# One pool of short-lived tiles, seven weight buffers, keys ordered by part, and a first norm turned by VectorE through DRAM

## The chip, the cores and the metric

The kernel runs on one core of a Trainium2 chip. A core has TensorE (PE in the profile; PEld is its weight load), VectorE (DVE), ScalarE (ACT), GpSimd (POOL) and SyncE (SP), which here only issues DMA transfers. Tiles lie in SBUF (128 partitions) or in PSUM, where matmuls write; PSUM has eight banks of 128 x 512 fp32 values. Transfers between DRAM and SBUF run on 16 DMA engines. The metric is the device time of one execution in microseconds.

## The reference

A transformer block in fp32 over x of shape (16, 512, 512): 16 batches of 512 tokens with 512 features. It has two halves, each a norm, a function, another norm and a residual.

```python
x = x + layernorm(attn(layernorm(x)))
x = x + layernorm(ffn(layernorm(x)))

# attn: 16 heads of 32; low-rank projections
q = h @ Wq_down.T @ Wq_up.T            # 512 -> 384 -> 512
c = h @ Wkv_down.T                     # 512 -> 128
k, v = c @ k_up[head], c @ v_up[head]  # 128 -> 32 per head
scores = q @ k.T * SCALE - slope[head] * |i - j|, causal
out = softmax(scores) @ v @ Wo.T

# ffn: weights are fp4 numbers, 8 to an int32, with a scale per group of 128
gate, up = h @ W_gate_up.T             # 512 -> 2 x 1408
y = (silu(gate) * up) @ W_down.T       # 1408 -> 512
y / sqrt(mean(y * y) + 1e-6)
```

## The kernel before

**The planner.** The code does not issue instructions where it describes them. Each piece of work is a `task`: the engines that may run it with an assumed busy time and end (`act`, `dve`, `pe`, `dma(us)`), a function that issues it, a due time in units of batches, and the tiles that it reads, writes or holds. `Plan.run` is a list scheduler. Again and again it takes the task that could start first by its assumed times, and among those the one with the earliest due time, looking at most half a batch ahead (`window=0.5`). What comes out is one fixed order of instructions per engine. On the chip every engine follows its order and waits on semaphores. A task that either ScalarE or VectorE can do (`either`) goes to the one that is free first in the plan. Buffers belong to named pools (`SLOTS`): `buf("g", ...)` takes a slot of pool `g` when its first task is placed and gives it back after its last; a later user of a slot waits for the earlier one's readers.

**The work of a batch.** A batch is four tiles of 128 tokens; attention has four groups (`g`) of four heads, and the queries are taken in four blocks (`qb`), each with (qb + 1) x 128 keys because of the causal mask.

- `first_norm`: `xl` is loaded, VectorE takes its statistics (L450), GpSimd the reciprocal root, ScalarE or VectorE normalizes in place. TensorE transposes the tile in four 128 x 128 pieces into a PSUM bank (`pta`, L490), and ScalarE or VectorE copies this into `xnT` (L439), which holds features on partitions and the 512 tokens along each.
- `project` (L600): `pc`, `pq`, `pk`, `pv` are the matmuls for c, q, k and v. Their results are copied out of PSUM.
- `scores`: four small matmuls side by side on rows of the array (`s`, L680); one VectorE operation adds the distance term and finds the maximum (L692); ScalarE does the exponential and the row sum (L707) into `p`.
- `turn`: brings `p` to keys on partitions, `pT`. In batch 0 by TensorE transposes (L773). In all later batches VectorE turns blocks of 32 x 32 in place (L790), one DMA stores the tile to DRAM (`pd`, L792), and four DMAs load it so that the blocks come to their places (`pT`, L797).
- `attend`: matmuls on columns of the array (`po`, L820), and a multiplication by the inverse row sums `rb`, which also go by way of DRAM (L741, L746).
- `tail`: the output projection (`pw`, L848), two norms, transposes (`ptf`) and a split of the result into two parts, `x2`.
- `ffn`: for each of 11 steps of 128 hidden features and for gate and up, a weight tile `wi` is loaded from DRAM (L891, 256 KB); each of four feature chunks gets two matmuls (`pg`, `pu`, L900); ScalarE scales and copies every first bank (L914), VectorE adds every second (L921), GpSimd adds the two halves (L927). ScalarE's tanh, one VectorE operation (L937) and a product on GpSimd (L941) make the hidden tile `hT`. Then 44 products `py` (L949), statistics, the last norm, and a store by GpSimd's queue.

In batch 0 the packed weights are unpacked as well and written to DRAM as `w_gu`.

**What sets the order around the change.** The feed-forward part of a batch is spread over the attention of the next: its due times begin 1.45 batches after the batch's start. So `wi`, `pd`, `pT`, `rb`, `xl` and `x` transfers are all issued by SyncE, one after another, in the planned order; one that waits holds those behind it. The short-lived tiles have pools of their own: `y` (3; also `rb`, scales and a raw load), `g`, `u`, `sum`, `th` (2 each). `wi` has four buffers.

Of the kernel before, what the change touches and what calls it, by code (L numbers as in the profile page):

```python
# [252 lines left out]
def dma(us):  # L253
    return 450.0, us * 1000.0
# [4 lines left out]
def attn_ffn_kernel(  # L259
# [38 lines left out]
        "xnT": (1, [P, ND, L], F32),  # L298
# [5 lines left out]
        "y": (3, [P, D], F32),  # L304
        "x2": (1, [P, 2, ND, L], F32R),
        "hT": (1, [P, NI, L], F32),
        "g": (2, [P, L], F32),
        "u": (2, [P, L], F32),
        "sum": (2, [P, L], F32),
        "th": (2, [P, L], F32),  # L310
        "wi": (4, [P, ND * P], F32R),
        **{f"p{qb}": (1, [P, (qb + 1) * P // HD, HPG, HD], F32) for qb in range(NT)},
        **{f"pT{qb}": (1, [P, qb + 1, HPG, HPG, HD], F32) for qb in range(NT)},
# [22 lines left out]


# [15 lines left out]
    dist = fixed([P, L], "dist")  # L353
# [10 lines left out]

    task({POOL: pool2(L)}, make_dist, -0.1, writes=[dist])

# [59 lines left out]
    raw = buf("y", "raw")  # L426
# [10 lines left out]

    def copy(e, dst, src):
        (nc.scalar.copy if e == ACT else nc.vector.tensor_copy)(dst, src)  # L439

    def either(n, extra=0.0):
        return {ACT: act(n, extra), DVE: dve(n, extra)}
# [12 lines left out]
    def norm(dst, src, rd, wr, tag, due, dur):  # L455

        st, mv, r, f = stats(src, tag, due)
        task({DVE: (700.0 + 150, 1000.0)}, f, due, reads=rd, writes=[st, mv])
        task({POOL: (1100.0, 1200.0)},
             lambda e: (rsqrt(r.t[:, 0:1], mv.t[:, 1:2], EPS_LN), shift(r, mv)), due,  # L460
             reads=[mv], writes=[r])
        scaled(dst, src, mv, r, rd, wr, due, dur)
# [87 lines left out]
    def unpack_gate_up(i):  # L550
        due = 0.15 + 0.06 * i
        words, high = unpack(gup, i * 16, NGU * P, i % (NI // 2) * 2, due)
        for half in range(2):
            wi = buf("th", f"wq_{i}_{half}")
            cols = slice(half * ND * P, (half + 1) * ND * P)
            task({ACT: act(ND * P)},
                 lambda e, wi=wi, cols=cols: nc.scalar.activation(
                     wi.t.bitcast(F32R), high()[:, cols], AF.Copy, scale=2.0**14),
                 due, reads=words, writes=[wi])
            task({SP: dma(2.6)},  # L560
                 lambda e, wi=wi, half=half: nc.sync.dma_start(w_gu[i, half], wi.t),
                 due, reads=[wi], writes=[(gu, (i, half))])

    def unpack_down(i):
        due = 0.85 + 0.06 * i
        sc = buf("y", f"sc_{i}")
# [13 lines left out]
    xnT = {}  # L580

    def first_norm(b, t):
        due = b - 0.3 + 0.06 * t
        if t == 0:
            xnT[b] = buf("xnT", f"xnT_{b}")
        xl, xn_t = xls[b, t], xnT[b]
        norm(lambda: xl.t, lambda: xl.t, [xl], [xl], f"a_{b}_{t}", due, dve(512, -100))
# [3 lines left out]
            lambda e: copy(e, xn_t.t[:, :, t * P : (t + 1) * P], blocks(pt.t)),  # L591
# [16 lines left out]
    def make_c(m):  # L608
        m.c = buf("cT", f"cT_{m.b}")
        project(  # L610
            m.c, None, lambda c: w_kv.t[:, c, :], lambda c: m.xn.t[:, c, :], ND,
# [4 lines left out]
    def make_q(m, g, due):  # L616
# [3 lines left out]
        def put(e, pm):  # L620
# [7 lines left out]
            lambda c: m.xn.t[:, c, :], ND, [w_q, m.xn, qscale],  # L628
# [3 lines left out]
    def make_k(m, g, due):  # L632
# [4 lines left out]
            lambda e, pm: copy(e, k.t, pm),  # L637
# [16 lines left out]
    def runs(ap):  # L654
        return ap.rearrange("p (b c) -> p b c", c=HD)

    def flat(ap):
        return ap.rearrange("p b j c -> p (b j c)")


    def part(m, p, j):
        if m.b == 0:
            ap = flat(p.t)
            w = ap.shape[1] // HPG
            return runs(ap[:, j * w : (j + 1) * w])
        return p.t[:, :, j, :]

    def scores(m, g, qb, due):
# [8 lines left out]
        def f(e):  # L677
            for j in range(HPG):
# [4 lines left out]
                    k.t[rows, :w],  # L683
# [5 lines left out]
        for j in range(HPG):  # L689
# [3 lines left out]
                    part(m, p, j),  # L693
                    runs(s[j].t[:, :w]),
                    runs(dist.t[:, L - w :]),
# [6 lines left out]
                due, reads=[s[j], dist], writes=[(p, j), (nmx, j)],  # L702
            )
        for j in range(HPG):
# [3 lines left out]
                    part(m, p, j), part(m, p, j), AF.Exp, bias=nmx.t[:, j : j + 1],  # L708
# [21 lines left out]
    def inverse(m, g, due):  # L730
        r = rowsums[g]
        d = rows_d[g]
        rb = m.rb[g] = buf("y", f"rb_{m.b}_{g}")
# [27 lines left out]
    def turn(m, g, qb, p, due):  # L761
        w = (qb + 1) * P
        row = w * HPG
        name = f"{m.b}_{g}_{qb}"
        p_t = buf(f"pT{qb}", f"pT_{name}")
        if m.b == 0:

            for j in range(HPG):
                pt = buf("bank", f"pt_{name}_{j}")

                def f(e, j=j, pt=pt):
                    for kb in range(qb + 1):
                        nc.tensor.transpose(  # L773
                            pt.t[:, kb * P : (kb + 1) * P],
                            flat(p.t)[:, j * w + kb * P : j * w + (kb + 1) * P],
# [7 lines left out]
                        e, p_t.t[:, : qb + 1, :, j, :],  # L783
                        pt.t[:, :w].rearrange("p (k a c) -> p k a c", a=HPG, c=HD),
# [3 lines left out]
            return p_t  # L788
        d = scratch[g, qb]
        task({DVE: dve(row, 0.07 * row)}, lambda e: nc.vector.transpose(flat(p.t), flat(p.t)),  # L790
             due, reads=[p], writes=[p])
        task({SP: dma(5.5 + w / 200)}, lambda e: nc.sync.dma_start(d.t, flat(p.t)), due,  # L792
             reads=[p], writes=[d])
        for i in range(HPG):
# [3 lines left out]
                    p_t.t[i * HD : (i + 1) * HD, : qb + 1],  # L798
                    bass.AP(
                        d.t.tensor, d.t.offset + i * P,  # L800
                        [[row, HD], [HPG * P, qb + 1], [HD * row, HPG], [1, P]],
# [4 lines left out]
        return p_t  # L806


    def attend(m, g, units, due):
# [5 lines left out]
        def f(e):  # L815
            for q, p_t, _ in units:
                for kb in range(q + 1):
                    for j in range(HPG):
# [4 lines left out]
                            p_t.t[:, kb, :, j, :],  # L823
# [14 lines left out]
    def tail(m, t, due):  # L838
# [5 lines left out]
        pm, y = buf("bank", f"pw_{b}_{t}"), buf("y", f"y_{b}_{t}")  # L844
# [35 lines left out]
    def ffn(m):  # L880
# [3 lines left out]
        for i in range(NI):  # L884
            accs = []
            for half, kind in enumerate("gu"):
                acc = buf(kind, f"{kind}_{b}_{i}")
                add = buf("sum", f"{kind}2_{b}_{i}")
                wi = buf("wi", f"wi_{b}_{i}_{half}")
                task({SP: dma(4.5)},  # L890
# [41 lines left out]
            th = buf("th", f"th_{b}_{i}")  # L932
# [11 lines left out]
        for t in range(NT):  # L944
# [34 lines left out]
            z, x = buf("th", f"z_{b}_{t}"), m.x[t]  # L979
# [9 lines left out]
    for b in range(B):  # L989
# [22 lines left out]
        for n in range(NG * NT):  # L1012
# [3 lines left out]
            units.append((qb, turn(m, g, qb, p, due + 2.2 * STEP), None))  # L1016
# [69 lines left out]
```

## Time and profile before

| | |
|---|---|
| median of 3 runs | 2503.35 us (2502.45 to 2506.34) |
| the profiled execution | 2499.75 us, span 2498.0 us |
| mean granted TensorE clock | 0.989 |
| TensorE busy | 2407.1 us, 13496 matmul instructions |
| VectorE, ScalarE, GpSimd busy | 1825.3, 1489.8, 1190.2 us |
| DMA | 487103 packets, 497.15 MB; SyncE's queue 71.8% of 16 engines' span |
| TensorE, 906 to 1057 us | 148.76 of 151.00 us busy |

An fp32 matmul is issued as two matmul instructions, so counts in the profile are doubled for `py`, `pw`, `pq`, `pc`, `pk`, `pv`, `s` and `po`. Matmuls are pipelined: one of 512 columns is shown with 592 ns, but eight `pq` in the chain take 3.43 us. So busy time is not a measure of TensorE at its peak, and the waits that it stood in are read beside it. A batch takes about 151 us in the middle of the span.

The page gives busy time by engine, the chain of work that ended last with the share of each line, groups of instructions with what ended the idle time before them, and DMA. Other views list who waited for whom, with the total, the number and the longest; SyncE's queue has its own list, marked SPq, and idle time there costs nothing unless a transfer behind it is late.

### The profile page before, as it was taken

Reading aid. Unit: us, or ns where it says so; the run is one execution under the profiler, and the core shown is the slowest. Engines: PE = TensorE matmul, PEld = TensorE weight load, DVE = VectorE, ACT = ScalarE, POOL = GpSimd, SP = SyncE. Lnnn points to the kernel's source line nnn. Section 1 sums busy time; section 2 is a strip of 40 time slices with the busy share of each in tenths; the row PEclk is TensorE's granted clock in tenths of the full one; section 3 lists DMA queues with packets and bytes.
Section 4 is the critical chain, followed back from the end, with each engine's and each line's share of the span. In section 5 each row is a group of like instructions: output and inputs, shape, how many; then the busy total and the mean of one; then the engine's idle time right before and its main releaser. Section 6 shows DMA issues by size and latency. Waiting matters only on the chain.

```text
span 2498.0 us, 42338 instructions
## 1 busy us (share of the span) xinstructions
PE 2407.1 (96%) x13496; PEld 1347.3 (54%) x13496; DVE 1825.3 (73%) x4216; ACT 1489.8 (60%) x3516; POOL 1190.2 (48%) x1518
## 2 busy tenths in 40 slices
PE   7989999999999999999999999999999999999988
PEld 3546455555555555465554645555455564555554
DVE  4897686877768777777777867687686786867764
ACT  5866565665656556565565656566575665655543
POOL 1035454454554454554444554454444554544565
PEclk9999999999999999999999999999999999999999
DMA  7588687786868778687786967868677786877821
GB/s 240 164 221 232 156 224 208 212 224 171 231 186 239 211 178 237 173 235 198 195 222 181 244 181 197 231 189 238 174 211 202 207 226 165 220 203 200 219 68 47
DMA packets 487103, 497.15 MB, mean 199 GB/s; under 512 B 41568, under 2 KB 383456, under 8 KB 479200
## 3 DMA queue, kind: packets, MB, share of 16 engines
q1 hardware_dynamic: 481760, 477.65, 71.8%
q0 software_dynamic: 5120, 16.78, 1.9%
q8 instruction: 109, 1.79, 0.3%
q14 instruction: 114, 0.93, 0.1%
HBM read 313.42 MB, written 180.88 MB: 198 GB/s over the span
## 4 chain that ended last, share of the span: by engine, by line
PE 80%; DMA 11%; DVE 3%; ACT 3%; SPq 1%; POOL 1%; issue 1%; POOLq 0%; DVEq 0%; ACTq 0%
PE py L949 22%; PE pu L900 11%; PE pg L900 10%; PE pw L848 9%; PE pq L600 8%; PE s L680 6%; PE po L820 5%; DMA wi<-w_gu 5%; DMA pT<-pd 2%; PE pc L600 2%; PE pv L600 2%; PE pk L600 2%; ACT p L707 1%; PE ptf L490 1%; DMA xl<-x_in 1%
## 5 line engine op out<-in xcount | busy, mean ns | idle before, releaser
L949 PE MATMUL py<-w_dn,hT 128*128 128x512 f32 x1408 | 709.4, 605 | 2.2 <-POOL hT L941 2.0
L707 ACT ACTIVATE p<-p,nmx 128x128 f32<-128x128 f32 (+3 forms) x1024 | 565.1, 554 | 224.1 <-DVE nmx L692 214.4
L692 DVE CUSTOM_DVE_ANT_0 p<-s,dist 128x128 f32<-128x128 f32 (+3 forms) x1024 | 440.9, 485 | 100.9 <-PE s L680 97.3
L900 PE MATMUL pg<-x,wi 128*128 128x512 f32 x1408 | 477.5, 463 | 28.6 <-DMA wi<-w_gu 19.9
L900 PE MATMUL pu<-x,wi 128*128 128x512 f32 x1408 | 448.6, 442 | 23.6 <-DMA wi<-w_gu 11.1
L927 POOL TENSOR_TENSOR g<-g,g 128x512 f32<-128x512 f32 x176 | 228.6, 1299 | 343.1 <-DVE g L921 342.6
L927 POOL TENSOR_TENSOR u<-u,u 128x512 f32<-128x512 f32 x176 | 249.9, 1420 | 293.9 <-DVE u L921 293.4
L790 DVE STREAM_TRANSPOSE p<-p 128x512 f32<-128x512 f32 x240 | 360.4, 1502 | 22.9 <-ACT p L707 22.7
L900 PEld LDWEIGHTS pg<-x,wi 128*128 128x128 f32 x1408 | 263.8, 192 | 190.8 <-issue 96.7
L949 PEld LDWEIGHTS py<-w_dn,hT 128*128 128x128 f32 x1408 | 250.3, 189 | 186.7 <-issue 145.0
L900 PEld LDWEIGHTS pu<-x,wi 128*128 128x128 f32 x1408 | 258.5, 189 | 166.8 <-issue 70.2
L921 DVE SCALAR_TENSOR_TENSOR u<-pu,s_gu,u 128x512 f32<-128x512 f32 x352 | 260.0, 745 | 108.3 <-ACT u L914 57.0
L914 ACT ACTIVATE u<-pu,s_gu 128x512 f32<-128x512 f32 x352 | 239.9, 684 | 153.8 <-PE pu L900 143.6
L914 ACT ACTIVATE g<-pg,s_gu 128x512 f32<-128x512 f32 x352 | 238.9, 683 | 145.5 <-PE pg L900 125.3
L921 DVE SCALAR_TENSOR_TENSOR g<-pg,s_gu,g 128x512 f32<-128x512 f32 x352 | 259.0, 740 | 90.6 <-ACT g L914 59.8
L941 POOL TENSOR_TENSOR hT<-th,u 128x512 f32<-128x512 f32 x176 | 228.6, 1301 | 75.4 <-DVE th L937 69.4
L600 PE MATMUL pq<-xnT,w_q 128*128 128x512 f32 x512 | 232.7, 597 | 1.3 <-ACT w_q L439 1.3
L680 PE MATMUL s<-kT,qT 32*128 32x512 f32 (+3 forms) x2048 | 228.5, 484 | 1.3 <-ACT qT L622 1.2
L848 PE MATMUL pw<-w_o,atT 128*128 128x512 f32 x512 | 229.1, 595 | 0.0
L707 ACT ACTIVATION_READ_ACCUMULATOR p<-p,nmx 128x1 f32 x1024 | 195.1, 191 | 0.0
L820 PE MATMUL po<-pT,v 128*32 128x128 f32 x5120 | 170.5, 279 | 3.7 <-DMA pT<-pd 3.7
L680 PEld LDWEIGHTS s<-kT,qT 32*128 32x128 f32 x2048 | 92.5, 183 | 150.2 <-issue 51.9
(92 smaller groups left out, 2446.8 us busy)
## 6 DMA issues: line engine op xcount, KB each, us to landing
wi<-w_gu SPq DMA_DIRECT2D x352, 256.0 KB
pd<-p SPq DMA_DIRECT2D x60, 1024.0 KB
pT<-pd SPq DMA_DIRECT2D x240, 256.0 KB
pd<-p SPq DMA_DIRECT2D x60, 768.0 KB
pT<-pd SPq DMA_DIRECT2D x240, 192.0 KB
pd<-p SPq DMA_DIRECT2D x60, 512.0 KB
pT<-pd SPq DMA_DIRECT2D x240, 128.0 KB
xl<-x_in SPq DMA_DIRECT2D x64, 256.0 KB
```

The lines of the kernel that those rows point to most:

```text
L600: nc.tensor.matmul(pm.t, lhs(c), rhs(c), start=c == 0, stop=c == n - 1)
L680: nc.tensor.matmul(s[j].t[:, :w], q.t[rows, qb * P : (qb + 1) * P], k.t[rows, :w], start=True, stop=True,)
L692: lambda e, j=j: nc.vector.tensor_tensor_reduce(part(m, p, j), runs(s[j].t[:, :w]), runs(dist.t[:, L - w :]), -SLOPES[g * HPG + j], 3.4e38 ...
L707: lambda e, j=j: nc.scalar.activation(part(m, p, j), part(m, p, j), AF.Exp, bias=nmx.t[:, j : j + 1], scale=-1.0, accum_out=sums.t[:, qb * ...
L790: task({DVE: dve(row, 0.07 * row)}, lambda e: nc.vector.transpose(flat(p.t), flat(p.t)), due, reads=[p], writes=[p])
L820: nc.tensor.matmul(po.t[j * HD : (j + 1) * HD, q * P : (q + 1) * P], m.v.t[:, kb, h * HD : (h + 1) * HD], p_t.t[:, kb, :, j, :], start=kb ...
L848: nc.tensor.matmul(pm.t, m.at.t[:, g, t * P : (t + 1) * P], w_o.t[:, g, :], start=g == 0, stop=g == NG - 1,)
L900: nc.tensor.matmul(pm.t, wi.t[:, c * P : (c + 1) * P], m.x2.t[:, 1 - n, c, :], start=n == 0, stop=n == 1,)
L914: lambda e, to=to, pm=pm, s=s: nc.scalar.activation(to.t, pm.t, AF.Copy, scale=s),
L921: lambda e, to=to, pm=pm, s=s: nc.vector.scalar_tensor_tensor(to.t, pm.t, s, to.t, ALU.mult, ALU.add),
L927: lambda e, acc=acc, add=add: nc.gpsimd.tensor_tensor(acc.t, acc.t, add.t, ALU.add),
L949: lambda e, i=i, t=t, pm=pm: nc.tensor.matmul(pm.t, h_t.t[:, i, t * P : (t + 1) * P], w_dn.t[:, i, :], start=i == 0, stop=i == NI - 1,),
```

## The change

Four edits, and what goes with them:

1. One pool `f` of eight tiles of 128 x 512 takes the place of `y`, `g`, `u`, `sum` and `th` (11 tiles); `dist`, which was a tile of its own, takes one of `f` and gives it back after batch 0. All that used the old pools takes from `f`.
2. `wi` has seven buffers instead of four, and the plan assumes that such a load takes 6.5 us instead of 4.5.
3. Keys by part. After batch 0 the keys are kept in the order (part i, block, key in the part), where part i of each block of 128 is its keys 32 i to 32 i + 31. The copy of k out of PSUM reorders them (`parts_first`), the distance term has a reordered copy (`by_part`), and the scores and `p` then stand with all keys of a part together. The four `pT` loads each take one part, and so read one run of (qb + 1) x 128 values where they read qb + 1 runs of 128. `po` reads `pT` through a matching view.
4. For every batch but the first, `first_norm` normalizes into a tile `ya` of pool `f`, in an order of blocks that lets VectorE's 32 x 32 transposes, one store to DRAM (`td`) and four loads put the tile into `xnT`. This replaces the TensorE transposes and the copy from PSUM. `xnT` is now laid out by blocks of 32 tokens, and the projections read it in runs of 32.

```diff
-        "xnT": (1, [P, ND, L], F32),
+        "xnT": (1, [P, L // HD, ND, HD], F32),
...
-        "y": (3, [P, D], F32),
+        "f": (8, [P, D], F32),
...
-        "g": (2, [P, L], F32),
-        "u": (2, [P, L], F32),
-        "sum": (2, [P, L], F32),
-        "th": (2, [P, L], F32),
-        "wi": (4, [P, ND * P], F32R),
+        "wi": (7, [P, ND * P], F32R),
...
+    def parts_first(ap):
+        return ap.rearrange("p (k i c) -> p i k c", i=HPG, c=HD)
...
     def first_norm(b, t):
...
+        mine = slice(t * HPG, (t + 1) * HPG)
+        if b > 0:
+            y, d = buf("f", f"ya_{b}_{t}"), turn_d[t]
+            norm(lambda: y.t.rearrange("p (i n c) -> p n i c", i=HPG, c=HD),
+                 lambda: xl.t.rearrange("p (n i c) -> p n i c", i=HPG, c=HD),
+                 [xl], [y], f"a_{b}_{t}", due, dve(512, -100), lambda: xl.t)
+            task({DVE: dve(D, 0.07 * D)}, lambda e: nc.vector.transpose(y.t, y.t), due,
+                 reads=[y], writes=[y])
+            task({SP: dma(6.0)}, lambda e: nc.sync.dma_start(d.t, y.t), due,
+                 reads=[y], writes=[d])
+            for i in range(HPG):
+                task(
+                    {SP: dma(7.0)},
+                    lambda e, i=i: nc.sync.dma_start(
+                        xn_t.t[i * HD : (i + 1) * HD, mine],
+                        bass.AP(d.t.tensor, d.t.offset + i * P,
+                                [[D, HD], [HD * D, HPG], [1, P]]),
+                    ),
+                    due, reads=[d], writes=[(xn_t, (t, i))],
+                )
+            return
...
-            lambda c: m.xn.t[:, c, :], ND, [w_q, m.xn, qscale],
+            lambda c: m.xn.t[:, :, c, :], ND, [w_q, m.xn, qscale],
...
-            lambda e, pm: copy(e, k.t, pm),
+            lambda e, pm: copy(
+                e, k.t if m.b == 0 else
+                k.t.rearrange("p (i k c) -> p i k c", i=HPG, c=HD),
+                pm if m.b == 0 else parts_first(pm)),
...
     def turn(m, g, qb, p, due):
...
                 lambda e, i=i: nc.sync.dma_start(
-                    p_t.t[i * HD : (i + 1) * HD, : qb + 1],
+                    p_t.t[i * HD : (i + 1) * HD, :row].rearrange("p (a n) -> p a n", a=HPG),
                     bass.AP(
-                        d.t.tensor, d.t.offset + i * P,
-                        [[row, HD], [HPG * P, qb + 1], [HD * row, HPG], [1, P]],
+                        d.t.tensor, d.t.offset + i * w,
+                        [[row, HD], [HD * row, HPG], [1, w]],
                     ),
                 ),
...
     def ffn(m):
...
-                acc = buf(kind, f"{kind}_{b}_{i}")
-                add = buf("sum", f"{kind}2_{b}_{i}")
+                acc = buf("f", f"{kind}_{b}_{i}")
+                add = buf("f", f"{kind}2_{b}_{i}")
                 wi = buf("wi", f"wi_{b}_{i}_{half}")
-                task({SP: dma(4.5)},
+                task({SP: dma(6.5)},
...
-            th = buf("th", f"th_{b}_{i}")
+            th = buf("f", f"th_{b}_{i}")
```

## The prediction

> **What bounds the kernel now.** I read the page first: busy shares, then the chain that ended last. After that came the waits of TensorE and of SyncE's DMA queue, the costly groups with shapes kept apart, and one stretch of the chain in order of time.
>
> ```profile
> span 2498.0 us, 42338 instructions
> PE 2407.1 (96%) x13496; PEld 1347.3 (54%) x13496; DVE 1825.3 (73%) x4216; ACT 1489.8 (60%) x3516; POOL 1190.2 (48%) x1518
> ...
> PE 80%; DMA 11%; DVE 3%; ACT 3%; SPq 1%; POOL 1%; issue 1%; POOLq 0%; DVEq 0%; ACTq 0%
> PE py L949 22%; PE pu L900 11%; PE pg L900 10%; PE pw L848 9%; PE pq L600 8%; PE s L680 6%; PE po L820 5%; DMA wi<-w_gu 5%; DMA pT<-pd 2%; PE pc L600 2%; PE pv L600 2%; PE pk L600 2%; ACT p L707 1%; PE ptf L490 1%; DMA xl<-x_in 1%
> ```
>
> TensorE is the bound: busy 96%, and 80% of the chain. Next stand the feed-forward weight loads (`wi`, 5%) and the turned probabilities (`pT`, 2%). The other engines have 27% or more of slack. So an edit pays if it shortens TensorE's own work or a wait that TensorE stands in; what it costs elsewhere is free as long as it is not late. The waits of TensorE, each with total us, times and longest:
>
> ```profile
> PE pg L900 <- DMA wi<-w_gu: 19.9, 12, 4.0
> PE pu L900 <- DMA wi<-w_gu: 11.1, 8, 3.0
> ...
> PE pu L900 <- ACT xnT L439: 4.8, 7, 0.7
> ...
> PE po L820 <- DMA pT<-pd: 3.7, 5, 1.5
> ...
> PE pg L900 <- DVE u L921: 2.3, 2, 1.2
> ```
>
> All rows of this view sum to 78 us; 31.0 of it is for `wi`. Why the loads are late shows in SyncE's queue:
>
> ```profile
> SPq L792 <- DVE p L790: 527.6, 140, 8.0
> SPq L797 <- DMA pd<-p: 144.4, 77, 6.8
> ```
>
> SyncE issues in order. A store `pd` that waits for VectorE's turn of `p` holds whatever is queued behind it, `wi` loads included, for up to 8.0 us. A stretch of the chain (start us, length us) shows the rates:
>
> ```profile
> 1069.19 2.04 PE pg L900 x8
> 1071.23 1.81 PE pu L900 x8
> ...
> 1079.91 7.58 DMA wi<-w_gu
> ...
> 1095.00 0.87 PE pta L490 x8
> ```
>
> In a burst a `wi` tile is used up in 1.81 to 2.04 us, and a load takes 7.58 us from issue to the matmul that it releases. With four buffers a slot freed now is needed again after the other three: 3 x 1.81 = 5.4 us, less than 7.58. The last line prices a transpose of the first norm: 0.87 / 8 = 109 ns.
>
> **The change part by part.** The sum is made against the profiled execution (2499.75 us, span 2498.0 plus 1.75). That is 3.6 us under the median of 2503.35; I carry the difference over to the median.
>
> *First norm off TensorE.* 15 of 16 batches lose their 16 transposes: 240 x 109 ns = 26.2 us of TensorE, all of it on the bound. The copies out of PSUM go too (60 of 64, 0.59 us each, nearly all ScalarE's), and with them four PSUM bank uses per batch. TensorE waited 4.8 us for banks that these copies held. I take all of it away; the bounds are 0 (another reader holds the bank next) and 4.8.
>
> It adds 60 VectorE transposes and DMAs: 60 stores `td` of 256 KB and 240 loads of 64 KB.
>
> ```profile
> L790 DVE STREAM_TRANSPOSE p<-p 128x512 f32<-128x512 f32 x60 | 42.1, 701 | 15.3 <-ACT p L707 15.2
> L490 PE MATMUL pta<-ident,xl 128*128 128x128 f32 x256 | 39.3, 283 | 7.6 <-ACT xl L472 7.1 <-DVE xl L475 0.6
> L439 ACT COPY xnT<-pta 128x512 f32<-128x512 f32 x57 | 32.6, 585 | 10.6 <-PE pta L490 10.6
> ```
>
> The same shape already runs 60 times on VectorE: +42.1 us. By the changed program's instruction order, choices between two engines also move: VectorE takes 26 more `v` copies and 9 more `x` copies (0.69 us each, 24 us) and loses some 24 `xnT`, `kT` and `qT` copies (17 us). VectorE goes to about 1875 us, 77% of a 2450 us span. Still covered by TensorE; if it were not, its 42 us would outweigh the 26.
>
> What waits anew: `pc`, the projection that opens a batch, now waits for a norm, a turn, a store and a load. The row nearest to that is `pT<-pd`: the same turn, store and load through DRAM on the same queue, 240 times, and TensorE waited for it 3.7 us in all. The lower end is a gain of 0.7, the one wait of `pc` for a copy into `xnT`. The upper end is one whole load in the open per batch, 15 x 7.58 = 114 us. The planner places the loads well ahead of `pc`, among `wi`, `pT` and `rb` issues, and `xnT` is free about 0.3 of a batch (some 45 us) before. I take +5, near the `pT` row.
>
> On SyncE's queue the 300 issues add 60 x 0.34 (as for `pd`) plus 240 x 0.61 us (the median issue of a `pT` load), about 167 us. The `td` stores also wait for VectorE: at the mean of `pd` (527.6 / 240 = 2.2 us) 132 us more of head-of-line blocking, with `wi`, `pT` and `rb` queued behind. What pays for it is the next two parts; what they leave is in the upper bounds. GpSimd's norm steps and output DMAs keep their number.
>
> *Keys by part.* A `pT` load reads one run per key part instead of one 512-byte run per block: for 1 to 4 blocks 128 packets each instead of 128, 256, 384 and 512. Over 240 loads of each size that is 122,880 packets instead of 307,200, for the same bytes. In the trace's packet records 512-byte packets take 40 ns and 2048-byte ones 103 ns. The `pT` loads then cost 16 engines about 550 us instead of 776, while `td` and its loads add some 127: DMA goes from 72% to about 68% of the span. Fewer pieces should also make issuing no dearer. TensorE's possible gain is its 3.7 us; I count 1. The new strides (16 runs of 32 in `xnT`) should cost nothing: `po` already reads runs of 32, and its columns go at the same rate. Batch 0 writes `p` contiguously and the later batches in runs of 32; VectorE's score operation takes 687 and 685 ns there at 512 keys, ScalarE's exponential 738 and 713, so runs of another length change nothing.
>
> *Seven `wi` buffers, planned for 6.5 us.* The cover becomes 6 x 1.81 = 10.9 us, above 7.58. A load behind an 8.0 us block can still be late. Of 31.0 us I take 25 away; bounds 0 and 31.
>
> *One pool of eight.* `y`, `g`, `u`, `sum`, `th` had 11 tiles and `dist` one; now eight serve all (seven in batch 0), plus the norm's new tile. A half-step pair uses five (g, its addend, u, its addend, th). Any free tile will do, so a long-held one (`rb`) no longer takes from a fixed few; but two half-step pairs in flight want ten. The price unseen in the trace is a late tile that holds ScalarE, then the PSUM bank, then TensorE. Lower end: a gain of 2.3, the row of a bank that waited for `u`. Upper end: one GpSimd add (1.42 us) in the open per step, 176 x 1.42 = 250. I take +8, near the low end, since TensorE's waits for the `g`/`u` workers are a few us now.
>
> Sum: -26.2 - 4.8 + 5 - 1 - 25 + 8 = -44, so 2456 against the profiled run and **2459** against the median (-1.8%).
>
> [...]
>
> **The rivals.**
> 1. *The loads stay late* (0.20). `wi` is held by the queue, not by buffers: SyncE waits up to 8.0 us on `pd`, and `td` adds such waits. Against it: 10.9 us of cover. Then the 25 falls out: -19, 2484.
> 2. *More goes than I count* (0.17). All `wi` and bank waits go, nothing new comes, and half of the other 42 us of recorded waits go with lighter DMA: -26.2 - 4.8 - 31 - 21 = -83, 2420.
> 3. *Slower: tiles run out* (0.15). GpSimd is already behind VectorE in long chains, and eight tiles cover about one and a half half-step pairs. At 0.5 us per step 88 instead of 8: +36, 2539. It decides from 0.30 us per step (52 / 176).
> 4. *Slower: the turned norm is late* (0.08). `xnT` has one buffer, and its last readers end before the loads may start. At 7.58 us per batch 114 instead of 5: +65, 2568. It decides from 3.3 us per batch (49 / 15).
>
> **How the numbers follow.** The forecast has 0.40; its own range, with 10 more or less of `wi` and of tiles, is 2435 to 2480. 2415 reaches beyond rival 2, and 2520 takes in rival 1 and the milder half of rivals 3 and 4. Outside stay their worse halves and a little below, under 0.2. This kernel can tell 0.2%, about 5 us, from no change. Faster: the forecast, rivals 1 (less 0.03) and 2, 0.74. Same: 0.05, from rival 1 and the mild ends of 3 and 4. Slower: 0.21, these two, with a wider reach for both.
>
> **What the profile after would show.** `pta` 16 instead of 256; a `td` store and `xnT` loads; VectorE near 77%; DMA packets near 340,000. If right: `wi` waits of TensorE under 10 us, a batch some 3 us shorter than the 151 now. Rival 1: `wi` still near 30 us. Rival 3: matmuls `pg`/`pu` waiting for ScalarE or VectorE, these for GpSimd. Rival 4: `pc` waiting for a DMA into `xnT`. What would prove the reading wrong: equal or shorter waits and yet no shorter span, or matmuls on the strided `xnT` slower than 592 ns.

## The result, and the profile after

The changed kernel takes 2487.97 us (median of 7 runs, 2480.22 to 2495.53), the kernel before 2505.96 beside it (2502.45 to 2507.88). The ratio is 0.9933 [0.9912, 0.9953]: 18 us or 0.7% faster, where 44 us had been forecast. It lies inside the range on record and outside the forecast's own one (2435 to 2480). The profiled execution took 2494.82 us at a mean granted clock of 0.982 (0.989 before).

The page of the changed kernel, span, busy time, chain by engine and line, DMA:

```profile
span 2492.8 us, 42456 instructions
PE 2383.0 (96%) x13256; PEld 1330.2 (53%) x13256; DVE 1886.9 (76%) x4296; ACT 1456.5 (58%) x3437; POOL 1178.7 (47%) x1518
PE 72%; DMA 11%; DVE 4%; ACT 1%; SPq 1%; issue 1%; POOL 1%; POOLq 0%; DVEq 0%
PE py L989 21%; PE pg L940 11%; PE pu L940 10%; DMA pT<-pd 8%; PE pq L634 7%; PE pw L888 7%; PE s L716 5%; PE po L860 5%; PE pv L634 2%; PE pc L634 2%; PE pk L634 1%; DMA wi<-w_gu 1%; DVE p L830 1%; DMA pd<-p 1%; DVE st_o L455 1%
DMA packets 345984, 528.62 MB, mean 212 GB/s; under 512 B 46368, under 2 KB 203936, under 8 KB 338080
q1 hardware_dynamic: 340640, 509.12, 73.4%
```

DMA has the same 11% of the chain as before, but another transfer has it: `wi` fell from 5% to 1%, `pT` rose from 2% to 8%. The waits of TensorE say the same (total us, times, longest):

```profile
PE po L860 <- DMA pT<-pd: 52.2, 15, 5.9
PE po L860 <- DMA rb<-rd: 8.3, 2, 4.2
PE pta L495 <- ACT xl L477: 7.1, 1, 7.1
...
PE pc L634 <- ACT xnT L334: 0.7, 1, 0.7
```

The `wi` rows, 31.0 us before, are gone. `po` waits 52.2 us for `pT` (3.7 before). The two waits that bear the name `rb`, 8.3 us, are waits for `pT` too: `po` does not read `rb`, and the semaphores that it waits on there are those of four `pT` loads (101 to 104 at 1581.46 us, of loads issued from 1570.07 to 1572.38 us). They are used again by later transfers (101 to 103 by `rb` loads issued from 1577.52 us on), and the view names the last one issued on them. The only wait of `pc`, where the forecast had looked for the new norm's price, is 0.7 us in batch 0. All rows sum to 94.9 us, before to 77.7. The part that was meant to change did, by the groups with shapes kept apart:

```profile
L605 DVE STREAM_TRANSPOSE ya<-ya 128x512 f32<-128x512 f32 x60 | 42.4, 707 | 3.5 <-ACT ya L477 2.6
L495 PE MATMUL pta<-ident,xl 128*128 128x128 f32 x16 | 4.2, 430 | 7.6 <-ACT xl L477 7.1 <-DVE xl L480 0.5
```

**Where the new wait is.** The trace has 13 stalls of `po` of 3.0 to 5.9 us, 59 us together. Twelve of them come once per batch, from 528 us on, always at one place: `po` of group 2, query block 3, whose four `pT` loads are the widest. (The other one, at 560 us, is of group 3.) SyncE's queue around one of them (start us, us, tile, how many in a row):

```profile
1551.96 4.94 SPq L612 DMA_DIRECT2D xnT<-td  x9
1557.00 0.38 SPq L882 DMA_DIRECT2D x<-x_in  x1
1557.42 1.87 SPq L837 DMA_DIRECT2D pT<-pd  x4
1559.39 0.85 SPq L832 DMA_DIRECT2D pd<-p  x2
1560.33 2.32 SPq L931 DMA_DIRECT2D wi<-w_gu  x1
...
1569.69 0.34 SPq L931 DMA_DIRECT2D wi<-w_gu  x1
1570.07 2.61 SPq L837 DMA_DIRECT2D pT<-pd  x4
```

In VectorE's timeline, the turn of the widest `p` of this group:

```profile
1553.66 2.31 DVE L830 STREAM_TRANSPOSE p<-p 128x2048 f32<-128x2048 f32 x1
```

The turn ended at 1555.97, and SyncE was in the middle of nine `xnT` loads of the next batch. The two `pd` stores behind them, the turned `p` in the second, went out at 1559.39 to 1560.24, about 4 us after the data were ready; the `pT` loads of this `p` began at 1570.07. In the twelve batches with the stall the store went out 3.5 to 9.1 us after its turn, in e1 below at most 0.4 us in the same batches. The chain in order of time shows who paid:

```profile
1560.33 9.28 DMA wi<-w_gu
...
1570.85 7.93 DMA pT<-pd
...
1578.80 2.61 DMA rb<-rd
...
1581.46 1.94 PE po L860 x32
```

The piece named `rb` is one of the two misnamed waits: the last of the four `pT` loads, issued at 1572.38, ended at 1581.32 by the semaphore that `po` waits on. The `xnT` loads stand in the way and are themselves on time; `po` pays. In the windows (us, then busy us of TensorE, its weight loads, VectorE, ScalarE, GpSimd; the granted clock, DMA's share, GB/s) the stall has a second price:

```profile
1572.00:1577.00 5.00, 5.00 (x44) 3.52 (x40) 4.36 (x11) 4.25 (x13) 1.44 (x2) 1.00 1.06 219
1577.00:1581.00 4.00, 0.24 (x12) 0.00 (x0) 2.03 (x3) 0.54 (x2) 1.26 (x1) 1.00 1.06 213
1581.00:1584.40 3.40, 2.94 (x35) 2.40 (x36) 0.00 (x0) 0.00 (x0) 0.00 (x0) 0.50 0.41 101
1584.40:1594.00 9.60, 9.60 (x35) 5.13 (x34) 8.19 (x15) 6.08 (x14) 3.80 (x3) 1.00 0.94 303
```

After the stall the granted clock is 0.50 for 3.40 us. Of the 13 stalls 12 were followed by 3.4 or 6.8 us at 0.50. Over the span, (1 - clock) x span is 45 us of lost clock, before 27.

### The profile page after: what moved, and what is told of

It reads as the page before. It is cut to its first block, busy times and chain, and to the rows that moved or that the text cites. A ratio compares the mean times of both kernels' runs of the same rounds, so it can differ in the third digit from the quotient of the medians.

```text
span 2492.8 us, 42456 instructions
## 1 busy us (share of the span) xinstructions
PE 2383.0 (96%) x13256; PEld 1330.2 (53%) x13256; DVE 1886.9 (76%) x4296; ACT 1456.5 (58%) x3437; POOL 1178.7 (47%) x1518
## 2 busy tenths in 40 slices
DMA packets 345984, 528.62 MB, mean 212 GB/s; under 512 B 46368, under 2 KB 203936, under 8 KB 338080
## 3 DMA queue, kind: packets, MB, share of 16 engines
q1 hardware_dynamic: 340640, 509.12, 73.4%
## 4 chain that ended last, share of the span: by engine, by line
PE 72%; DMA 11%; DVE 4%; ACT 1%; SPq 1%; issue 1%; POOL 1%; POOLq 0%; DVEq 0%
PE py L989 21%; PE pg L940 11%; PE pu L940 10%; DMA pT<-pd 8%; PE pq L634 7%; PE pw L888 7%; PE s L716 5%; PE po L860 5%; PE pv L634 2%; PE pc L634 2%; PE pk L634 1%; DMA wi<-w_gu 1%; DVE p L830 1%; DMA pd<-p 1%; DVE st_o L455 1%
## 5 line engine op out<-in xcount | busy, mean ns | idle before, releaser
L989 PE MATMUL py<-w_dn,hT 128*128 128x512 f32 x1408 | 694.0, 606 | 1.3 <-POOL hT L981 1.2
L940 PE MATMUL pg<-x,wi 128*128 128x512 f32 x1408 | 463.9, 452 | 2.3 <-DVE x L910 1.4
L940 PE MATMUL pu<-x,wi 128*128 128x512 f32 x1408 | 430.1, 434 | 4.6 <-DVE atT L874 3.2
L728 DVE CUSTOM_DVE_ANT_1 p<-s,by_part 128x128 f32<-128x128 f32 x720 | 262.0, 419 | 149.5 <-PE s L716 148.7
L989 PEld LDWEIGHTS py<-w_dn,hT 128*128 128x128 f32 x1408 | 257.2, 191 | 210.6 <-issue 168.6
L967 POOL TENSOR_TENSOR u<-u,u 128x512 f32<-128x512 f32 x176 | 234.4, 1332 | 253.2 <-DVE u L961 252.9
L967 POOL TENSOR_TENSOR g<-g,g 128x512 f32<-128x512 f32 x176 | 235.8, 1340 | 197.5 <-DVE g L961 191.9
L860 PE MATMUL po<-pT,v 128*32 128x128 f32 x5120 | 179.8, 286 | 64.4 <-DMA pT<-pd 52.2
L716 PE MATMUL s<-kT,qT 32*128 32x128 f32 (+3 forms) x2048 | 224.0, 481 | 3.6 <-DVE atT L874 2.2
L860 PEld LDWEIGHTS po<-pT,v 128*32 128x32 f32 x5120 | 138.0, 113 | 124.5 <-issue 69.6
```

The lines of the kernel that those rows point to most:

```text
L716: nc.tensor.matmul(s[j].t[:, :w], q.t[rows, qb * P : (qb + 1) * P], first_keys(m, k.t[rows], w), start=True, stop=True,)
L728: lambda e, j=j: nc.vector.tensor_tensor_reduce(part(m, p, j, w), s[j].t[:, :w] if b == 0 else s[j].t[:, :w].rearrange("p (i n) -> p i n", ...
L860: nc.tensor.matmul(po.t[j * HD : (j + 1) * HD, q * P : (q + 1) * P], m.v.t[:, kb, h * HD : (h + 1) * HD], view()[:, :, j, kb, :], start=kb ...
L940: nc.tensor.matmul(pm.t, wi.t[:, c * P : (c + 1) * P], m.x2.t[:, 1 - n, c, :], start=n == 0, stop=n == 1,)
L967: lambda e, acc=acc, add=add: nc.gpsimd.tensor_tensor(acc.t, acc.t, add.t, ALU.add),
L989: lambda e, i=i, t=t, pm=pm: nc.tensor.matmul(pm.t, h_t.t[:, i, t * P : (t + 1) * P], w_dn.t[:, i, :], start=i == 0, stop=i == NI - 1,),
```

## The experiments

Ratios are to the kernel before, run beside each kernel (its medians were 2501 to 2506 us, so a difference between kernels that were not run side by side is good to some 5 us). "PE waits" is the sum of all rows of TensorE's waits.

| run | what differs | us | ratio [95%] |
|---|---|---|---|
| e1 | after, first norm on TensorE | 2421.18 | 0.9672 [0.9656, 0.9689] |
| e2 | after, four `wi` | 2519.88 | 1.0062 [1.0035, 1.0090] |
| e3 | before, first norm through DRAM | 2529.01 | 1.0111 [1.0087, 1.0134] |
| e4 | after, `xnT` loads a quarter as large | 2476.78 | 0.9902 [0.9881, 0.9923] |
| e5 | after, `td`, `xnT` on ScalarE's queue | 2528.66 | 1.0105 [1.0076, 1.0134] |
| e6 | after, `td`, `xnT` on GpSimd's queue | 2444.32 | 0.9767 [0.9749, 0.9786] |
| e7 | before, pool of eight and seven `wi` | 2432.72 | 0.9721 [0.9707, 0.9736] |
| e8 | e1, four `wi` | 2452.98 | 0.9807 [0.9791, 0.9823] |
| e9 | before, pool of eight | 2464.66 | 0.9846 [0.9832, 0.9861] |
| e10 | before, pool of eleven | 2497.69 | 0.9977 [0.9958, 0.9996] |
| e11 | e1, 240 tiny loads on SyncE's queue | 2527.10 | 1.0097 [1.0075, 1.0119] |
| e12 | after, half of the norm through DRAM | 2419.28 | 0.9665 [0.9648, 0.9682] |
| e13 | after, `xnT` loads behind a `pd` store | 2493.30 | 0.9949 [0.9932, 0.9967] |
| e14 | after, `xnT` loads behind `pT` loads | 2497.50 | 0.9972 [0.9962, 0.9983] |

### What is each part worth?

**e1: everything but the norm's new way.**

```diff
-        if b > 0:
+        if False:
```

> The changed kernel with its first norm put back on TensorE in every batch; pool, seven wi buffers and keys by part stay. Theory T (burst): once a batch the four td stores and sixteen xnT loads run beside pd, pT and wi and make the pT of group 2 late; without them TensorE's wait on pT falls from 52 us to under 10, the transposes bring back 26 us and their bank waits 5, so about 2488 - 52 - 10 + 31 = 2457 us (0.980 of before). Rivals W (the deeper wi prefetch crowds out pT), K (the longer pT runs are slower) and O (the planned order is too tight): the wait stays near 50 us and the time is about 2519 us (1.005).

2421 us. With TensorE's 240 transposes back, the kernel is 67 us faster than the changed one; 31 had been expected. Its waits for `pT` and its clock:

```profile
PE po L860 <- DMA pT<-pd: 0.9, 2, 0.7
```

```profile
core 0: 2415.3 us, clock 0.995
```

PE waits are 32.0 us, and a batch takes 145.6 us (from one batch's `pw` to the next, mean of 13), in the changed kernel 150.6, before 151.25. The profiled spans differ by 77.5 us. Idle time is 62.9 of it, lost clock 33 (45 against 12); the transposes saved take 26 off, at the forecast's price. That makes 70, so nearly all of the difference is named. The norm through DRAM thus cost about 67, and the other three edits together brought about 82. Both figures hold an effect of the planned order too, which differs in all three kernels.

**e3: the norm's new way alone**, on the kernel before (the edit's fourth part, with `ya` from pool `y` and `xnT` in blocks of 32).

```diff
+        if b > 0:
+            y, d = buf("y", f"ya_{b}_{t}"), turn_d[t]
...
+            task({SP: dma(6.0)}, lambda e: nc.sync.dma_start(d.t, y.t), due,
...
+            return
```

> The kernel before with one edit alone: the first norm turned by VectorE and by way of DRAM (its tile ya from pool y). Theory T: TensorE gains 31 us and waits some 50 us more on pT, with the clock lost after these waits about 10: 2506 - 31 + 60 = 2535 us (1.012 of before). Rivals W and K: no new wait on pT, 2475 us (0.988).

It costs 28 us there too, and another transfer pays. TensorE's waits in e3:

```profile
PE pg L929 <- DMA wi<-w_gu: 60.4, 28, 4.7
PE pu L929 <- DMA wi<-w_gu: 11.4, 7, 3.6
```

71.8 us for `wi` where the kernel before had 31.0; `pT` has only 5.3. It fits that with four `wi` buffers the loads that stand behind the new transfers and have least time in hand are `wi`, and with seven `pT`.

**e2: the changed kernel with four `wi` buffers.**

```diff
-        "wi": (7, [P, ND * P], F32R),
+        "wi": (4, [P, ND * P], F32R),
...
-                task({SP: dma(6.5)},
+                task({SP: dma(4.5)},
```

> The changed kernel with four wi buffers and 4.5 us again. Theory T: the wait on pT stays at 40 to 55 us and the waits on wi come back with about 30 us: 2519 us (1.005 of before). Rival W: the wait on pT falls under 10 us, the waits on wi come back: 2488 - 52 + 31 = 2467 us (0.984).

The time is near what was expected, the place is not: `pT` did not keep its wait. It fell under 10 us, as the rival W had it, whose time was 53 us too low. TensorE's waits in e2:

```profile
PE pg L940 <- DMA wi<-w_gu: 38.3, 18, 3.6
...
PE pu L940 <- DMA wi<-w_gu: 6.7, 9, 1.8
PE po L860 <- DMA pT<-pd: 6.3, 3, 4.7
```

Same transfers and another planned order: 45.0 us for `wi`, 6.3 for `pT`. What the norm's loads displace is a matter of the order; that they displace something is not.

**e8: e1 with four `wi` buffers** (the edit of e2, made in e1).

> The changed kernel with its first norm on TensorE and four wi buffers planned for 4.5 us: pool of eight and keys by part are left. If the buffers carry the gain: TensorE's waits on wi come back with 30 us or more and the time is 2421 + 31 + 14 of lost clock = 2466 us or more (0.985 of before). If the pool and the keys carry it: within 10 us of 2421 (0.968 to 0.972).

2453: the three more buffers are worth 32 us beside the pool of eight (2452.98 - 2421.18). But TensorE waits for `wi` only 3.4 us here. Of the 33 us between the profiled spans all waits of TensorE are 9.0 (41.0 against 32.0); the clock is the same (0.996 and 0.995), and 23.6 us is time shown as busy (2393.4 against 2369.8, the same 13496 matmul instructions; 17.5 us of it in `pu`, 448.3 against 430.8). Why the same matmuls, in another order, take that much longer is open.

**e7: pool of eight and seven `wi` on the kernel before**, without keys by part (and `dist` on its own).

```diff
-        "y": (3, [P, D], F32),
+        "f": (8, [P, D], F32),
...
-        "g": (2, [P, L], F32),
-        "u": (2, [P, L], F32),
-        "sum": (2, [P, L], F32),
-        "th": (2, [P, L], F32),
-        "wi": (4, [P, ND * P], F32R),
+        "wi": (7, [P, ND * P], F32R),
```

> The kernel before with the pool of eight and the seven wi buffers (6.5 us) alone: first norm on TensorE and keys as before; dist keeps a tile of its own. Its planned order should be that of the run with the norm on TensorE, with longer pT issues and four times the packets. If keys by part carry little: 2421 to 2433 us (0.968 to 0.972 of before). If they carry the gain beyond the 31 us of wi waits: 2455 or more (0.981).

2433. e1 has the same planned order on TensorE and keys by part beside it, so keys by part are worth 11 us (2432.72 - 2421.18); e9 below and e8 differ by them too, 12 us. TensorE's waits fall by as much, 42.6 us to 32.0, 3.2 of it in the `pT` row.

**e9: the pool of eight alone** (e7 with `wi` left at four and 4.5 us).

> The kernel before with one edit: y, g, u, sum and th (11 tiles) become one pool of eight; four wi buffers, old keys, norm on TensorE, dist a tile of its own. If the shared pool itself brings the gain that pool and keys had together (2453 us): 2453 plus the 11 us of the keys = 2464 us (0.985 of before). If eight tiles cost what the prediction counted (+8 us): 2510 (1.003).

2465, a gain of 38 us: not a price, but the largest gain of the three. The `wi` waits fall with `wi` untouched:

```profile
PE pg L896 <- DMA wi<-w_gu: 5.3, 6, 2.2
```

(7.4 us with the row of `pu`, 31.0 before. All waits of TensorE fall from 77.7 to 47.7 us, the lost clock from 27 to 12, of 36 us between the spans.)

**e10: the same with eleven tiles**, as many as the five pools had.

```diff
-        "f": (8, [P, D], F32),
+        "f": (11, [P, D], F32),
```

> The same with a pool of eleven shared tiles, as many as the separate pools had. If sharing is what helps and three tiles fewer cost nothing: the same as the run with eight, 2464 us (0.985), within 5 us. If fewer tiles help (by another order): near 2501 here. If tiles were short with eight: faster than that run by 5 us or more.

2498, a gain of 6 us. So it's not the sharing that brings the 38 but eight tiles in place of eleven (no other number was run). TensorE waits for `wi` in e10 as long as in the kernel before:

```profile
PE pg L896 <- DMA wi<-w_gu: 21.7, 14, 3.1
PE pu L896 <- DMA wi<-w_gu: 10.7, 7, 2.7
```

Eight and eleven give different planned orders. From a `wi` load's issue to its first use the 5th percentile is 5.7 us before, 5.8 in e10 and 7.1 in e9, for loads issued between 600 and 2300 us (the shortest 3.0, 4.6 and 6.1; earlier in the span e10 and e9 have some of 2.7). It fits that fewer tiles keep half-steps from running ahead in bursts, so that the same four `wi` buffers are used up less fast; that is argued from these lead times, no run isolates it.

### Why does the norm's new way cost 67 us?

Candidates: the bytes of its loads, the issue of so many transfers on SyncE's queue, VectorE's added work, or the place where they stand.

**e4: `xnT` loads with one block of 32 tokens instead of four**, in the same planned order.

```diff
-                        xn_t.t[i * HD : (i + 1) * HD, mine],
+                        xn_t.t[i * HD : (i + 1) * HD, t * HPG : t * HPG + 1],
                         bass.AP(d.t.tensor, d.t.offset + i * P,
-                                [[D, HD], [HD * D, HPG], [1, P]]),
+                                [[D, HD], [HD * D, 1], [1, P]]),
```

> The changed kernel with the same order of instructions, but each xnT load moves only a quarter (16 KB instead of 64 KB; three quarters of xnT keep older values, so the attention of later batches is computed from wrong inputs). It leaves 46 MB... no compute is left out. Theory T by bytes (16 DMA engines are full for some 20 us a batch): the wait on pT falls from 52 us to under 15, about 2440 us (0.974 of before). If the jam is one of issues and of places in the queue, not of bytes: the wait stays near 50 us and the time near 2488.

The bytes left out are 240 x 48 KB = 11.8 MB (the 46 in the expectation is a slip). TensorE's wait in e4:

```profile
PE po L867 <- DMA pT<-pd: 51.3, 17, 4.9
```

51.3 against 52.2 us, and 2477 against 2488. With a quarter of the bytes and of the packets SyncE takes as long to issue them (419 ns in the median of the 240 loads, 430 in the changed kernel). The bytes that the loads leave out are some 11 us of the 67; those of the stores `td` stayed.

**e5 and e6: `td` and `xnT` on another engine's queue.**

```diff
-            task({SP: dma(6.0)}, lambda e: nc.sync.dma_start(d.t, y.t), due,
+            task({ACT: (100.0, 6000.0)}, lambda e: nc.scalar.dma_start(d.t, y.t), due,
...
-                    {SP: dma(7.0)},
-                    lambda e, i=i: nc.sync.dma_start(
+                    {ACT: (100.0, 7000.0)},
+                    lambda e, i=i: nc.scalar.dma_start(
```

(e6: `POOL: (700.0, ...)` and `nc.gpsimd` in these places.)

> The changed kernel with the td stores and the xnT loads issued and planned on ScalarE's queue instead of SyncE's; bytes and number stay. Theory Q (places in SyncE's order): the pd stores of groups 2 and 3 no longer stand behind these 300 issues, TensorE's wait on pT falls from 52 us under 10, and with the clock lost after these waits the time is about 2488 - 52 - 20 = 2416 us (0.965 of before), plus what the issues cost ScalarE. Rival T (the traffic as such, or the tight planned order): the wait stays over 40 us and the time near 2488 (0.994).

> The same as the run before with GpSimd's queue in place of ScalarE's. Theory Q: the wait on pT under 10 us, about 2416 us (0.965) plus what GpSimd's products hT lose behind issues that wait (GpSimd is 47% busy); if these lose 0.3 us a step, 53 us, 2469. Rival T: the wait on pT over 40 us.

On ScalarE's queue the `pT` wait falls to 5.9 us, and ScalarE, which does its own work in order, is late instead: matmuls wait for its copies. TensorE's waits in e5:

```profile
PE pu L940 <- ACT g L954: 12.6, 7, 5.1
PE pg L940 <- ACT u L954: 12.0, 3, 4.1
PE pg L940 <- ACT kT L334: 11.6, 7, 2.8
```

On GpSimd's queue the kernel takes 2444, 44 us less than the changed one. TensorE's wait in e6:

```profile
PE po L860 <- DMA pT<-pd: 18.9, 16, 4.6
```

VectorE's 60 turns, the bytes and the chain from turn to load are all still there, so about two thirds of the 67 us go with SyncE's queue (the planned order is another too, so this is no exact price). e6 stays 23 us above e1, with 18.9 of waits for `pT`; what makes those is open. One issue is small, 430 ns in the median for an `xnT` load, where the `pT` load in the chain took 7.93 us to land. But the issues stand in front of later transfers and add up (nine in a row took 4.94 us above): with 300 of them off SyncE's queue the kernel was 44 us faster.

**e11: e1 with 16 loads of 128 bytes per batch on SyncE's queue**, which nobody reads.

```diff
+    idle = fixed([P, NT * HPG], "idle")
+
+    def bystanders(m, due):
+        for n in range(NT * HPG):
+            i = n % HPG
+            task({SP: dma(7.0)},
+                 lambda e, n=n, i=i: nc.sync.dma_start(
+                     idle.t[i * HD : (i + 1) * HD, n : n + 1],
+                     x_in[m.b, i * HD : (i + 1) * HD, n : n + 1]),
+                 due, reads=[m.q[NG - 1]], writes=[(idle, n)])
...
+                if g + 2 == NG and b + 1 < B:
+                    bystanders(m, b + 0.7)
```

> The run with the norm on TensorE (2421 us), and beside it sixteen loads a batch of 4 bytes to each of 32 partitions on SyncE's queue, into a tile that nobody reads; in the plan they become ready when the last q of a batch is through, as the xnT loads do. They move 0.03 MB in all. Theory Q (places in SyncE's order and its eight transfers in flight): pd stores of groups 2 and 3 wait 2 us or more longer, TensorE's wait on pT comes up from 1 us to 15 or more, 2440 us or more (0.975). If only transfers of some size or the waits of the td stores matter: within 6 us of 2421 (0.968 to 0.970).

2527: 240 transfers of 0.03 MB in all cost 106 us. The victim is not the expected `pT` (3.5 us). The waits of all engines in e11:

```profile
DVE st_a L455 <- DMA xl<-x_in: 75.8, 16, 6.8
```

```profile
PE pu L951 <- DVE nmx L739: 33.7, 12, 4.0
```

An `xl` load is late, VectorE stands at its statistics once per batch, and what is queued behind on VectorE holds TensorE. The clock is 0.975, 63 us lost. So added transfers with no data to speak of can come with a cost above that of the whole norm; but the added tasks also change the planned order of the others, so the 106 aren't the price of the issues alone.

**e13 and e14: the same order on every other engine, the 16 loads of a batch moved on SyncE's queue**: behind the `pd` store of group 2, block 3 (e13), or behind its last `pT` load (e14). The planned tasks are issued in the planned order except those loads, which are held:

```diff
-    for t in plan.run(window=0.5):
+    batch_of = {id(t): k[0] for k, t in loads.items()}
+    opens = {id(t): k[0] + 1 for k, t in gate.items() if k[1:] == (2, 3)}
+    opened, held = {1}, {}
...
+    for t in plan.run(window=0.5):
+        n = batch_of.get(id(t))
+        if n is not None and n not in opened:
+            held.setdefault(n, []).append(t)
+            continue
+        issue(t)
+        n = opens.get(id(t))
+        if n is not None:
+            opened.add(n)
+            for x in held.pop(n, []):
+                issue(x)
```

> The changed kernel with the same plan, the same transfers and the same order on TensorE, VectorE, ScalarE and GpSimd; on SyncE's queue alone the sixteen xnT loads of the next batch are moved back behind the pd store of group 2, block 3. Theory Q (what stands ahead of that store in SyncE's order): the store goes out when its turn is done, TensorE's wait on pT falls from 52 us to under 15 and the clock lost from 46 us to under 25: about 2488 - 40 - 20 = 2428 us (0.970 of before). If the traffic as such or the tightness of the plan makes pT late: the wait stays over 40 us and the time within 10 us of 2488 (0.990 to 0.998).

> The same, with the xnT loads behind the last pT load of group 2, block 3. Theory Q: as the run before, with the pT loads of that block not behind the xnT loads either: wait on pT under 8 us, 2420 us (0.967). If the loads then come too late for pc: TensorE waits for xnT in pc, 3 us or more a batch.

e13 missed what was expected. The store now goes out as soon as the turn ends, but the loads stand between `pd` and its `pT` loads, which follow 14.8 us after the store instead of 8.8. SyncE's timeline, and TensorE's wait, in e13:

```profile
1558.93 2.75 SPq L832 DMA_DIRECT2D pd<-p  x2
1561.73 9.62 SPq L612 DMA_DIRECT2D xnT<-td  x16
...
1575.90 2.01 SPq L837 DMA_DIRECT2D pT<-pd  x4
```

```profile
PE po L860 <- DMA pT<-pd: 57.7, 19, 5.3
```

In e14 the `pT` wait is 3.7 us: in the same planned order, the place of these loads alone takes it away. `pc` waited for the later loads twice, 5.8 us in all, not in every batch. But now the `rb` loads stand behind, `atT`, which needs `rb`, is late, and TensorE waits for that:

```profile
PE s L716 <- DVE atT L874: 41.0, 12, 4.7
```

`rb` was late in the changed kernel already, where TensorE stood behind `pT`. VectorE's wait for it there:

```profile
DVE atT L874 <- DMA rb<-rd: 76.8, 14, 7.8
```

and in e1:

```profile
DVE atT L874 <- DMA rb<-rd: 2.3, 3, 1.3
```

2493 and 2498, where 2428 and 2420 had been expected, and no better than 2488. From 350 us on the sixteen take SyncE 8.6 to 12.2 us in one stretch in e13 and 11.0 to 14.0 in e14, and at both places something with less time in hand stands behind. Part of that is waiting: SyncE's transfers use eight semaphores in turn (100 to 107, all 2362 issues in the trace of the changed kernel), and an issue waits until the transfer eight places before it has landed: there the `rb` loads at 1577.52, 1578.80 and 1580.31 us went out 0.02 us after the last landings of `pT` loads on their semaphores. `xnT` issues waited 23.9 us for `pT` loads in the changed kernel, 25 times, and 68.8 us in e14, 88 times. So an added transfer takes one of eight places as well as the time of its issue; no run separates the two.

**e12: two of a batch's four tiles by way of DRAM.**

```diff
-        if b > 0:
+        if b > 0 and t < 2:
```

> The changed kernel with only the first two of the four tiles of a batch turned by way of DRAM; the other two on TensorE. Half the issues: theory Q with a queue that has room for half gives TensorE 13 us and no new wait on pT, 2421 - 13 = 2408 us (0.963 of before). If the cost goes with the number: half way between 2421 and 2488, 2455 (0.981).

2419, as fast as e1 within the intervals, with 2.9 us of waits for `pT`. Eight loads do fit; half of the 26 us of transposes is off TensorE, but of the 13 us expected from it 2, which the intervals do not tell from nothing, are gained. Both e1 and e12 are 3.3% faster than the kernel before and some 2.7% faster than the changed one.

## Why the prediction was wrong

The direction was right and the sum was not: it had two errors of opposite sign. The forecast counted -26 for the norm's new way (-26.2 - 4.8 + 5) and -18 for the rest (-1 - 25 + 8). Measured they are about +67 and -82.

- **TensorE's transposes, -26.2.** The work went as counted: 16 `pta` instead of 256, and VectorE's 60 turns take 42.4 us (42.1 forecast). That they fell away is seen in the counts; that 26 us came with it is not shown by itself: e12, with half of them gone and nearly no new wait, is 2 us from e1. VectorE went to 1886.9 us and 76% (1875 and 77% forecast), and no row of TensorE's waits in the changed kernel names the turn.
- **Bank waits, -4.8.** The row `pu <- ACT xnT` is gone, as taken. But it is gone in e1 too, where the copies out of PSUM are back, so the norm's new way is not shown to have earned it.
- **"What waits anew", +5: the step that failed.** The right row was read (`pT`, 3.7 us), with the right question, but it was asked only of the new transfers' own reader, `pc` (0.7 us measured). The readers of what is queued behind them weren't priced: `po` for `pT`, 60.5 us with the two waits named `rb`, and the clock after the stalls, 33 us more lost than in e1. "167 us" of issue and "132 us" of head-of-line wait were totals over 2498 us of span, set against nothing. Both came out lower (132 us of issue; `td` stores waited 61.6 us for their turn), and the cost came all the same, because the issues come as 16 in one phase of a batch, up to nine in a row (4.94 us above), in front of `pT` and `rb` loads that have no such time in hand. "What pays for it is the next two parts" put no number on it.
- **Keys by part, -1.** The packets went to 345,984 (340,000 forecast), and strided `xnT` is as fast as said. The tile's view (min/median/max ns) of the changed kernel, `pq` by way of the strided tile (590/592/1061 in the kernel before):

```profile
L634 PE MATMUL pq<-xnT,w_q x512: 590/592/1062, 30.6 to 2290.2; 128*128 128x512 f32 x171
```

  But DMA went to 73.4% on SyncE's queue, not 68%: a 2048-byte packet took 121 ns instead of the 103 used, and a 1536-byte one 116. And the gain is 11 us, more than the 3.7 us of waits that the step took as its bound. The median issue of a `pT` load on SyncE fell from 610 to 430 ns (583 to 429 us in all); "fewer pieces should also make issuing no dearer" was where the gain was to be looked for.
- **Seven `wi`, -25.** TensorE waits for `wi` nowhere now, and the shortest way from a load's issue to its use, for loads issued between 600 and 2300 us, went from 3.0 to 10.3 us. The 32 us (e8) are near the step's upper bound of 31, but not by its mechanism: the pool of eight alone had left only 7.4 us of `wi` waits (e9) to take away.
- **Pool of eight, +8.** Wrong in sign: -38 (e9). The step priced a late tile on the engines and did not ask what order the planner makes of fewer tiles. Rival 3, tiles run out, has the same error; no wait in the changed kernel shows it.
- **Rival 1**, loads late in the queue, gave 2484 and is nearest in time. It had the mechanism, SyncE's head of line, and the wrong victim: `wi` is on time, `pT` is not. That its number is near is luck: it too counted -26 for the norm's new way and +8 for the pool. **Rival 4**, the turned norm late for `pc`, did not happen.

## What to carry to other kernels

When a change adds transfers to an in-order queue, price them in the stretch of the batch where they are issued, and price what stands behind them, not what reads them: count the issues in that phase, multiply by the issue time, and compare with the time in hand of each transfer that follows. To a stall of TensorE add the half-rate time that may follow it: here it was 3.4 or 6.8 us at a granted clock of 0.50 after 12 of 13 stalls of 3.0 to 5.9 us. And in a kernel whose order comes from a planner, an added or removed buffer is a new order: run each part alone before adding up its gains.

## What the hardware showed that was not expected

Stalls cost more than their length here. Of 13 stalls of `po` of 3.0 to 5.9 us (59 us), 12 were followed by 3.4 or 6.8 us at a granted clock of 0.50: 7 x 3.4 + 5 x 6.8 us at half rate, 29 us of lost time. The half-rate stretches in the traces of the kernel before and the changed kernel are 3.4 us long or two or three times that, save the last one of a trace. The length of a stall does not tell by itself whether one follows: in the kernel before, stalls of 2.3 us (333 us) and 2.6 us (484 us) were followed by 3.4 us at 0.50, while the one of 3.0 us at 528 us in the changed kernel was not. What the traces do show is a grid. In the clock records of both kernels all half-rate stretches of a trace (11 and 18) begin whole multiples of 3.413 us apart. Cut along this grid, between 100 and 2400 us, the two traces have some 1300 pieces at full clock. All 22 in which TensorE is shown idle for 0.58 or more of the piece were followed by half rate; of the others two were (idle for 0.48 and 0.10). So it fits that a stall counts by how much of one fixed 3.4 us stretch it leaves idle.

The size of a transfer hardly mattered to the queue that issued it: with a quarter of the bytes an `xnT` load took SyncE 419 ns in the median instead of 430 (e4), and a kernel with 16 more loads of 128 bytes per batch was 106 us slower (e11, whose planned order changed too).
